# A four-layer graph network on one core: targets' positions and a zero in PSUM, a sort with a predicated copy held behind its group's messages, 64-row products in layer 2, and one 480-column product per slot in layer 2's sums

## The chip, the cores and the metric

The kernel runs on one core of a Trainium2 chip. One core has five engines with an instruction stream each: TensorE (PE; its weight loads are listed apart as PEld), VectorE (DVE), ScalarE (ACT), GpSimd (POOL, which here issues the indirect DMAs) and SyncE (SP, which here issues the direct DMAs). The metric is the device time of one launch in microseconds (us); "before" is the median of ten runs.

## The reference

A graph has N = 6250 nodes with 160 features each (64 scalars, 32 vectors of 3) and E = 100,000 edges, sorted by target `dst`. Four layers follow each other, each as `x = x + layer(relu(layernorm(x)))`. Layers 0, 1 and 3 gather by source and sum by target; layer 2 gathers by target and sums by source. Cut to what matters:

```python
# layers 0, 1 and 3 (W: small two-layer network of the edge's features)
w0, w1, w2, w3 = split(W(edge_features))
e0, e1 = h0[src], h1[src]                     # node features after a linear map
m0a = w0 * e0 * y0                            # y0, y1: edge_attr_4[:, :1], [:, 1:]
m0b = w3 * einsum('eui,ei->eu', e1, y1)
m1a = (w1 * e0)[:, :, None] * y1[:, None, :]
m1b = w2[:, :, None] * (e1 * y0[:, :, None])
n = segment_sum(concat(m0a, m0b, m1a, m1b), dst)      # 384 columns
# layer 2
sh1 = SQRT3 * edge_attr_3 / norm(edge_attr_3)
xs, xv = s[dst], v[dst]
out0a, out0b = w0 * xs, w3 * dot(xv, sh1)
out1a, out1b, out1c = w1 * xs * sh1, w2 * xv, w4 * cross(xv, sh1)
agg = segment_sum(concat(...), src)                   # 480 columns
```

After each sum stand linear maps of the nodes, in layer 2 a silu and a gate, in layer 3 a rotation by an angle.

## The kernel before

**Tiles.** An edge tile is 128 edges, one to a partition; there are TT = 784. WT = 14 tiles make a window (NW = 56 windows), two windows a unit (NU = 28 units), and up to G = 4 tiles a group, of which a layer has 196. Because edges are sorted by target, a window's edges reach few nodes. Within a window the even tiles hold the first half of its edges and the odd tiles the second half, so each kind reaches a run of under 64 nodes (HN = 64): a "half window".

**Prologue** (up to 165 us). `Fast.prologue` counts edges per bucket of sources, and writes tables that stay in SBUF: `self.loc` [128, 784], each edge's target relative to its half window's first node; `self.column`, for joining the two halves of a window; and `self.plus_w` (the line is `nc.vector.tensor_scalar(self.plus_w, pw[:, 0, :], iota_p, None, op0=ALU.add)`), for each window the node number that each of 128 partitions stands for.

**Layers 0, 1 and 3** are `edges(li)`, a loop over the 196 groups with work prepared ahead. For a group:

- SP loads per unit `rt` (attributes and source number of each edge, line 1236) and `ft` (edge features); POOL gathers the sources' rows from the table in HBM, one indirect DMA for each tile (L1277, 784 in a layer), six groups ahead into eight buffers `ge`.
- `hidden` and `edge_weights` make the weights: PE `ph` and `pw` (L1293 in layer 3, L1300 in layers 0 and 1), ACT copies them to `ws` (L1304, L1306).
- `messages` (L1309) is DVE's work: per unit one copy of three attribute rows into the PSUM tile `yls` (L1313); per group the comparison `oh` of an iota with `self.loc` (L1319), the products L1330, L1333, L1336, L1337 and L1338 and the reduction L1331. `msg` has 384 columns and 64 of scratch.
- PE multiplies `oh` (64 columns as weights) by `msg` and adds up in PSUM (`pg`, L1394), even tiles in the upper half of the partitions, odd ones in the lower. At the end of a window ACT copies `pg` out, and the generator `nodes` starts: `nodes_out` (L1051: ACT's copy `at` L1069, DVE's L1073 that carries the border of two windows, PE's `po` L1080 and L1082) and then `nodes_in` of the next layer (L982: norm, with `inv_sqrt` L966 to L975, maps, and the store of the next table rows). Each running generator is advanced by two steps in every group:

```python
            live = [n for n in live if not (next(n, True) or next(n, True))]
            if li < 2 and i % 3 == 0:
                next(self.sort, None)
```

**The sort.** Layer 2 needs each edge's place in the order of sources. `positions` (L1142) is a generator that makes it on DVE during layers 0 and 1, a step in every third group. For each of BK + 1 = 54 buckets it compares (L1166), scans with a running sum (L1168, over 784 columns, with the zeros `zeros_b` in SBUF as the second operand), yields, multiplies (L1171), adds (L1172) and yields. Whatever is left after layer 1 is run at once. The framework's scheduler orders each engine's instructions when it builds the program: by their place in it, but an instruction whose data and buffers are free by the scheduler's reckoning can be put ahead of others that wait. So the steps do not run just where they are written: from 388 us on the scans' starts lie 30 to 60 us apart through layer 0, then seven of them lie between 1583 and 1621 us, at the border to layer 1, and the next is at 1981.

**Layer 2, messages** are `messages2` (L1411). Per window `select` (L1438) loads on SP's queue 128 rows of the table, `tb` (L1443), from the window's first node on, whose number SP reads into a register (`self.at`), and the targets of its 1792 edges to all 128 partitions, `dt` (L1445), and compares them on DVE with `plus_w` (L1447) to the matrix `oh` [128 nodes, 14, 128 edges]. Per group PE makes `pw` (L1468, with 64 rows, from two halves of the partitions by turns) and gathers by a product, `pe` (L1479, one PSUM tile, one buffer):

```python
                nc.tensor.matmul(pe[:, k, :160], lhsT=oh[:, (t0 + k) % WT, :], rhs=tb, start=True, stop=True)
```

ACT copies `pe` to `ev` and `row` (L1484 to L1486) and two smaller pieces to `row` (L1487, L1488); DVE makes the rest of `row` (L1497 to L1506); POOL scatters each tile's 128 records of 390 numbers (1560 B) to `rec2` in HBM at the sorted places (L1509, 784 indirect DMAs). `row` has five buffers.

**Layer 2, sums** are `sums2` (L1543): for each of 53 buckets of 120 nodes, groups of up to 4 slots of 128 records. SP loads a group's records into `rt` [128, 4, 390] (L1570, 12 buffers, 8 groups ahead), DVE takes the places `loc` out of it (L1573), compares (`oh`, L1601) and makes 288 columns of `msg` (L1605, L1607); PE adds up 480 columns per slot in two products with the same weights:

```python
                nc.tensor.matmul(pg[:, 0:192], lhsT=oh[:, k, :], rhs=rt[:, k, 0:192], start=first, stop=end,
                                 skip_group_check=True)
                nc.tensor.matmul(pg[:, 192:480], lhsT=oh[:, k, :], rhs=msg[:, k, :], start=False, stop=end,
                                 skip_group_check=True)
```

These are L1611 and L1613; at a bucket's end ACT copies `pg` out by four copies (L1621 to L1624), and the node generators run as in the other layers.

## Time and profile before

| | us |
|---|---|
| median of 10 runs | 6640.2 |
| lowest, highest | 6571.16, 6687.38 |
| profiled execution, its own time | 6601.84 |
| its span, first to last instruction | 6600.0 |
| mean granted TensorE clock in it | 0.804 of full |

The stages follow each other almost without overlap, so the span can be cut at the times where one stage's lines end and the next one's begin: prologue 0 to 165, layer 0 to 1587, layer 1 to 3110, layer 2's messages to 4368, its sums to 5178, layer 3 to 6600. The profile has a row of digits for each engine over 40 slices of 165 us, the busy share in tenths; a line of TensorE's granted clock; and one of the traffic. The costliest groups of instructions are listed with line, engine, operation, tiles (out<-in) and count, then total busy us, mean ns of one, and the idle time just before them with what ended most of it. For example:

```profile
L1394 PE MATMUL pg<-msg,oh 128*64 128x384 f32 x4704 | 1190.1, 632 | 251.9 <-issue 114.4
L1337 DVE TENSOR_TENSOR msg<-msg,yls 128x768 f32<-128x768 f32 x588 | 554.9, 944 | 0.0
```

The first says that the 4704 passes of layers 0, 1 and 3's sums (two for each tile) kept PE busy for 1190.1 us, and that PE idled 251.9 us in front of them. The second, that DVE's product L1337 took 944 ns on average. A row of the timeline has the start in us, the length, engine, line, operation and tiles, and in brackets the idle time ahead of it with what ended it; "x8" there means eight instructions in one row.

### The profile page before, as it was taken

What the parts mean: (1) busy time and instruction counts of PE and PEld (TensorE: products, weight loads), DVE (VectorE), ACT (ScalarE), POOL (GpSimd) and SP (SyncE); (2) the same over time, 40 slices, a digit from 0 to 9 for tenths busy, and PEclk for the clock granted to TensorE, in tenths of its full rate; (3) what the DMA queues carried; (4) which work ended last, traced back from release to release, by engine and by line L of the source; (5) the groups of instructions that cost most, each with busy time, mean ns of one, the idle gap of its engine ahead of it and who ended that gap; (6) DMA issues with size and microseconds to landing.
All of it is one profiled execution on the core that took longest, in us unless ns stands there. A gap on an engine that the chain in (4) does not pass through costs nothing. (4 is left out here: it accounts for less than half of the span.)

```text
span 6600.0 us, 77043 instructions
## 1 busy us (share of the span) xinstructions
PE 5029.0 (76%) x22084; PEld 3072.0 (47%) x22084; DVE 4217.7 (64%) x11655; ACT 2084.0 (32%) x6858; POOL 3269.5 (50%) x3143
## 2 busy tenths in 40 slices
PE   6688888887678878776665666669999677877677
PEld 4344444444344444443443444458888433433333
DVE  5567777767456767555666666667777466655556
ACT  5333333333233333333333332312222233322222
POOL 0566666653555556552666766620000365555554
PEclk9788888877687788777777777789999777767777
DMA  3322222222222222222655555567777222222221
GB/s 89 95 74 69 72 71 73 69 57 59 60 70 75 72 70 77 69 60 66 226 197 190 202 191 193 179 229 249 236 235 233 67 67 63 64 61 59 61 58 40
DMA packets 371211, 733.89 MB, mean 111 GB/s; under 512 B 69677, under 2 KB 249098, under 8 KB 370650
## 3 DMA queue, kind: packets, MB, share of 16 engines
q0 software_dynamic: 163072, 349.43, 18.4%
q1 hardware_dynamic: 207122, 379.11, 18.3%
q8 instruction: 180, 2.95, 0.2%
q14 instruction: 253, 2.07, 0.1%
q10 hardware_dynamic: 584, 0.33, 0.0%
HBM read 519.59 MB, written 209.08 MB: 110 GB/s over the span
## 5 line engine op out<-in xcount | busy, mean ns | idle before, releaser
L1277 POOL DMA_INDIRECT ge<-table,rt x2352 | 2424.3, 1031 | 2823.8 <-DMA skip<-sk 829.1
L1394 PE MATMUL pg<-msg,oh 128*64 128x384 f32 x4704 | 1190.1, 632 | 251.9 <-issue 114.4
L1509 POOL DMA_INDIRECT rec<-row,edge_to x784 | 844.5, 1077 | 455.8 <-issue 249.7
L1304 ACT ACTIVATE ws<-pw,rt 128x96 f32<-128x96 f32 x2352 | 693.6, 347 | 1058.7 <-DVE msg L1338 214.2
L1300 PE MATMUL pw<-w_w2y,hh 100*128 100x192 f32 x3136 | 741.7, 379 | 142.4 <-ACT ws L1306 120.2
L1300 PEld LDWEIGHTS pw<-w_w2y,hh 100*128 100x128 f32 x3136 | 588.1, 219 | 406.6 <-ACT ws L1306 209.6
L1394 PEld LDWEIGHTS pg<-msg,oh 128*64 128x64 f32 x4704 | 335.7, 164 | 867.6 <-issue 505.2
L1073 DVE TENSOR_TENSOR at<-at 96x4 f32<-96x4 f32 x165 | 27.1, 164 | 907.6 <-ACT at L1069 769.1
L1479 PE MATMUL pe<-tb,oh 128*128 128x160 f32 x1568 | 377.5, 385 | 284.0 <-ACT row L1486 210.9
L1337 DVE TENSOR_TENSOR msg<-msg,yls 128x768 f32<-128x768 f32 x588 | 554.9, 944 | 0.0
L1266 PE MATMUL ph<-ft,w_w1r 12*100 12x512 f32 (+1 forms) x784 | 419.6, 713 | 160.7 <-ACT hh L1269 86.4
L1613 PE MATMUL pg<-msg,oh 128*120 128x288 f32 x1668 | 540.6, 405 | 0.0
L1479 PEld LDWEIGHTS pe<-tb,oh 128*128 128x128 f32 x1568 | 295.1, 241 | 457.5 <-ACT row L1486 309.8
L1269 ACT ACTIVATE hh<-ph 100x1024 f32<-100x1024 f32 (+1 forms) x336 | 268.5, 799 | 719.2 <-remote 208.8
L1333 DVE TENSOR_TENSOR msg<-ws,ge 128x512 f32<-128x512 f32 x588 | 400.8, 682 | 54.6 <-ACT ws L1306 54.6
L1611 PE MATMUL pg<-rt,oh 128*120 128x192 f32 x1668 | 409.3, 327 | 27.3 <-DMA rt<-rec 27.3
L1502 DVE TENSOR_TENSOR row<-pw,ev 128x512 f32<-128x512 f32 x196 | 135.1, 689 | 426.4 <-ACT row L1488 339.9
L1306 ACT COPY ws<-pw 128x192 f32<-128x192 f32 x1176 | 386.4, 329 | 0.0
L1611 PEld LDWEIGHTS pg<-rt,oh 128*120 128x120 f32 x1668 | 297.6, 183 | 115.3 <-issue 28.1
L1331 DVE TENSOR_REDUCE dot<-pr 128x128 f32<-128x384 f32 x588 | 343.0, 583 | 0.1
L1330 DVE TENSOR_TENSOR pr<-ge,yls 128x384 f32<-128x384 f32 x588 | 318.4, 541 | 29.0 <-DMA ge<-table,rt 25.0
L1293 PE MATMUL pw<-w_w2d,hh 64*128 64x192 f32 x1568 | 289.6, 404 | 47.8 <-remote 36.3
(486 smaller groups left out, 7729.5 us busy)
## 6 DMA issues: line engine op xcount, KB each, us to landing
rt<-rec SPq DMA_DIRECT2D x208, 780.0 KB
dt<-in_dst_w_dram SPq DMA_DIRECT2D x56, 896.0 KB
ge<-table,rt POOLq DMA_INDIRECT x2352
ft<-in_ft_dram SPq DMA_DIRECT2D x56, 512.0 KB
ft<-in_ft_dram SPq DMA_DIRECT2D x28, 896.0 KB
xt<-x SPq DMA_DIRECT2D x168, 82.0 KB
rec<-row,edge_to POOLq DMA_INDIRECT x784
rt<-in_rec_dram SPq DMA_DIRECT2D x84, 112.0 KB
```

The source lines that it names most:

```text
L1266: nc.tensor.matmul(ph[:, i], lhsT=w1[r : r + K, :], rhs=ft[r : r + K, 4 * P * (j // 2) :][:, : 4 * P], start=True, stop=True)
L1277: nc.gpsimd.indirect_dma_start(out=ge[:, k, :], out_offset=None, in_=self.table[li], in_offset=bass.IndirectOffsetOnAxis(ap=rt[:, G * g + ...
L1300: nc.tensor.matmul(pw[:, i, :192], lhsT=hh[:, k + i, :], rhs=w2, start=True, stop=True)
L1304: nc.scalar.activation(ws[:, k0 + i, 0:96], pw[:, i, 0:96], AF.Copy, scale=rt[:, G * g + k0 + i, 0:1])
L1306: nc.scalar.copy(ws[:, k0 : k0 + m, 96:192], pw[:, :m, 96:192])
L1333: tt(msg[:, :, AW - 64 : AW + 64].rearrange("p g (k u) -> p g k u", k=2), ws.rearrange("p g (k u) -> p g k u", k=2)[:, :, :, 0:64], e0[:, ...
L1337: tt(mvec[:, :, :, 0:64], by3(t1, 64), yv[:, :, :, None].to_broadcast([P, n, 3, 64]), ALU.mult)
L1394: nc.tensor.matmul(pg[half], lhsT=oh[:, k, :], rhs=msg[:, k, :AW], start=t % WT < 2, stop=t % WT >= WT - 2)
L1479: nc.tensor.matmul(pe[:, k, :160], lhsT=oh[:, (t0 + k) % WT, :], rhs=tb, start=True, stop=True)
L1509: d = nc.gpsimd.indirect_dma_start(out=self.rec2, out_offset=bass.IndirectOffsetOnAxis(ap=self.edge_to[:, t0 + k : t0 + k + 1], axis=0), i ...
L1611: nc.tensor.matmul(pg[:, 0:192], lhsT=oh[:, k, :], rhs=rt[:, k, 0:192], start=first, stop=end, skip_group_check=True)
L1613: nc.tensor.matmul(pg[:, 192:480], lhsT=oh[:, k, :], rhs=msg[:, k, :], start=False, stop=end, skip_group_check=True)
```

## The change

It touches every stage.

- **Prologue:** `plus_w` is computed so that partitions 0 to 63 stand for the 64 nodes from the first half window's first node on, and partitions 64 to 127 for those of the second half window.
- **Sort:** the scan's second operand is one zero in PSUM, read as a broadcast, and not `zeros_b` in SBUF. The multiplication and the addition become one copy under a predicate. A step is issued with `tc.issue_after(last.ins)`: its instructions stand behind the last message operation of the group in whose turn the step falls.
- **Layers 0, 1 and 3:** the PSUM tile of the attributes (now `bank`) has a fourth row per tile, the targets' places, copied once per unit; the comparison `oh` reads it there.
- **Layer 2's messages:** `select` makes two table loads of 64 rows and two target loads, of 896 edges to 64 partitions each, and one comparison of half as many columns. The products `pe` use 64 rows: even tiles the upper half of the partitions, odd tiles the lower. Slots of the PSUM tile are permuted, so that the two halves write to banks of their own; ACT's copies read through a view that undoes it.
- **Layer 2's sums:** `rt` has room for 288 columns in front of each record. The load lands behind them, DVE writes the messages into them, and one product of 480 columns takes the place of the two. ACT's copies at a bucket's end have other offsets.

```diff
-        nc.vector.tensor_scalar(self.plus_w, pw[:, 0, :], iota_p, None, op0=ALU.add)
...
+        nc.vector.scalar_tensor_tensor(self.plus_w, column, -1.0, pw[:, 0, :], op0=ALU.add, op1=ALU.add)
...
-            nc.vector.tensor_tensor_scan(cum, hit, self.zeros_b, self.off[:, b : b + 1], op0=ALU.add,
+            nc.vector.tensor_tensor_scan(cum, hit, self.zero.to_broadcast([P, TT]), self.off[:, b : b + 1], op0=ALU.add,
...
-            nc.vector.tensor_mul(cum, cum, hit)
-            nc.vector.tensor_add(pos, pos, cum)
+            nc.vector.copy_predicated(pos, hit.bitcast(mybir.dt.uint16), cum)
...
-    def at(self, k, most=N):
-
-        return self.nc.values_load(self.first[0:1, 2 * k : 2 * k + 1], engines=[mybir.EngineType.SP], min_val=0, max_val=most,
+    def at(self, k, most=N, half=0):
+
+        return self.nc.values_load(self.first[0:1, 2 * k + half : 2 * k + half + 1], engines=[mybir.EngineType.SP], min_val=0, max_val=most,
...
-        yls = p_y.tile([P, 2, 3, 2 * WT], F32, name="yls")
+        bank = p_y.tile([P, 8 * 2 * WT + 1], F32, name="bank")
+        yls = bank[:, : 8 * 2 * WT].rearrange("p (u c t) -> p u c t", u=2, c=4)
+        self.zero = bank[:, 8 * 2 * WT :]
+        nc.vector.memset(self.zero, 0.0)
...
-                nc.vector.tensor_copy(yl, rt[:, :, 1:4].rearrange("p t c -> p c t"))
+                nc.vector.tensor_copy(yl[:, 0:3], rt[:, :, 1:4].rearrange("p t c -> p c t"))
+                nc.vector.tensor_copy(yl[:, 3], self.loc[:, 2 * WT * u : 2 * WT * u + 2 * WT])
...
-            t0 = 2 * WT * u + G * g
...
-               self.loc[:, t0 : t0 + n, None].to_broadcast([P, n, HN]), ALU.is_equal)
+               yl[:, 3, gs, None].to_broadcast([P, n, HN]), ALU.is_equal)
...
-            yv = yl[:, :, gs].rearrange("p c t -> p t c")
+            yv = yl[:, 0:3, gs].rearrange("p c t -> p t c")
...
-            tt(mvec[:, :, :, 64:96], e1, by3(ws[:, :, 64:96], 32), ALU.mult)
-            return oh, msg
+            last = tt(mvec[:, :, :, 64:96], e1, by3(ws[:, :, 64:96], 32), ALU.mult)
+            return oh, msg, last
...
-            oh, msg = messages(u, g)
+            oh, msg, last = messages(u, g)
...
-                next(self.sort, None)
+                with tc.issue_after(last.ins):
+                    next(self.sort, None)
...
-            n = min(WT, TT - WT * k) * P
-            at = self.at(k)
...
-            nc.sync.dma_start(tb, self.table[2][ds(at, P), :])
-            dt = ld.tile([P, WT * P], I32, name="dt", bufs=2)
-            nc.sync.dma_start(dt[:, :n], self.a["dst_w"][k : k + 1, :n].to_broadcast([P, n]))
-            oh = ld.tile([P, WT, P], F32, name="oh", bufs=3)
-            nc.vector.tensor_scalar(oh.rearrange("p t e -> p (t e)")[:, :n], dt[:, :n], self.plus_w[:, k : k + 1], None,
+            dt = ld.tile([P, WT // 2 * P], I32, name="dt", bufs=2)
+            for h in range(2):
+                rows = slice(HN * h, HN * h + HN)
+                nc.sync.dma_start(tb[rows], self.table[2][ds(self.at(k, half=h), HN), :])
+                nc.sync.dma_start(dt[rows], self.a["dst_w"][2 * k + h : 2 * k + h + 1, :].to_broadcast([HN, WT // 2 * P]))
+            oh = ld.tile([P, WT // 2, P], F32, name="oh", bufs=3)
+            nc.vector.tensor_scalar(oh.rearrange("p t e -> p (t e)"), dt, self.plus_w[:, k : k + 1], None,
...
+
...
-                nc.tensor.matmul(pe[:, k, :160], lhsT=oh[:, (t0 + k) % WT, :], rhs=tb, start=True, stop=True)
+                h, rows = k % 2, slice(HN * (k % 2), HN * (k % 2) + HN)
+                nc.tensor.matmul(pe[:, 2 * h + k // 2, :160], lhsT=oh[rows, (t0 + k) % WT // 2, :], rhs=tb[rows],
+                                 start=True, stop=True)
+            pe = pe.rearrange("p (h t) c -> p t h c", h=2)
+            pair = lambda v: v.rearrange("p (t h) c -> p t h c", h=2)
...
-            pe = pe[:, :n]
...
-            nc.scalar.copy(ev[:, :, 0:160], pe[:, :, 0:160])
-            nc.scalar.copy(ev[:, :, 160:224], pe[:, :, 64:128])
-            nc.scalar.copy(row[:, :, 294:390], pe[:, :, 64:160])
+            nc.scalar.copy(pair(ev[:, :, 0:160]), pe[:, :, :, 0:160])
+            nc.scalar.copy(pair(ev[:, :, 160:224]), pe[:, :, :, 64:128])
+            nc.scalar.copy(pair(row[:, :, 294:390]), pe[:, :, :, 64:160])
...
-            rt = ld.tile([P, G, RW], F32, name="rt")
-            nc.sync.dma_start(rt[:, :m, :],
+            rt = ld.tile([P, G, 288 + RW], F32, name="rt")
+            nc.sync.dma_start(rt[:, :m, 288:],
...
-            nc.vector.tensor_scalar(loc[:, :m], rt[:, :m, 261], float(-BN * b), None, op0=ALU.add)
+            nc.vector.tensor_scalar(loc[:, :m], rt[:, :m, 288 + 261], float(-BN * b), None, op0=ALU.add)
...
-            rt = rt[:, :n]
+
+            msg, rt = rt[:, :n, 0:288], rt[:, :n]
+            row = rt[:, :, 288:]
...
-            msg = wk.tile([P, G, 288], F32, name="msg", bufs=3)[:, :n]
...
-            tt(msg[:, :, 0:192].rearrange("p g (c u) -> p g c u", c=3), by3(rt[:, :, 192:256], 64),
-               rt[:, :, 256:259, None].to_broadcast([P, n, 3, 64]), ALU.mult)
+            tt(msg[:, :, 0:192].rearrange("p g (c u) -> p g c u", c=3), by3(row[:, :, 192:256], 64),
+               row[:, :, 256:259, None].to_broadcast([P, n, 3, 64]), ALU.mult)
...
-               rt[:, :, 294:390].rearrange("p g (c u) -> p g c u", c=3), by3(rt[:, :, 262:294], 32), ALU.mult)
+               row[:, :, 294:390].rearrange("p g (c u) -> p g c u", c=3), by3(row[:, :, 262:294], 32), ALU.mult)
...
-                nc.tensor.matmul(pg[:, 0:192], lhsT=oh[:, k, :], rhs=rt[:, k, 0:192], start=first, stop=end,
-                                 skip_group_check=True)
-                nc.tensor.matmul(pg[:, 192:480], lhsT=oh[:, k, :], rhs=msg[:, k, :], start=False, stop=end,
-                                 skip_group_check=True)
+                nc.tensor.matmul(pg, lhsT=oh[:, k, :], rhs=rt[:, k, 0:480], start=first, stop=end)
...
-            nc.scalar.copy(vecs[:, :, 0:64], comp(192, 64))
-            nc.scalar.copy(vecs[:, :, 64:96], comp(384, 32))
-            nc.scalar.copy(vecs[:, :, 96:128], comp(0, 32))
-            nc.scalar.copy(acc[:, 384:480], pg[:, 96:192])
+            nc.scalar.copy(vecs[:, :, 0:64], comp(0, 64))
+            nc.scalar.copy(vecs[:, :, 64:96], comp(192, 32))
+            nc.scalar.copy(vecs[:, :, 96:128], comp(288, 32))
+            nc.scalar.copy(acc[:, 384:480], pg[:, 384:480])
...
-    a["dst_w"] = by_tile(i["dst"], 1 << 20).reshape(NW, WT * P)
+    a["dst_w"] = np.append(i["dst"], np.full(TT * P - E, 1 << 20, np.int32)).reshape(2 * NW, WT // 2 * P)
```

## The prediction

> **What bounds it now.** I read the page's head first, then busy time in six stretches cut where one stage's lines end and the next one's begin, then the groups of instructions, waits and timelines inside each stretch.
>
> ```profile
> PE 5029.0 (76%) x22084; PEld 3072.0 (47%) x22084; DVE 4217.7 (64%) x11655; ACT 2084.0 (32%) x6858; POOL 3269.5 (50%) x3143
> ...
> 165.00:1587.00 1422.00, 1166.62 (x5071) 655.67 (x5072) 988.93 (x2708) 518.30 (x1622) 840.21 (x784) 0.83 0.28 72
> 1587.00:3110.00 1523.00, 1184.41 (x4799) 649.79 (x4797) 926.79 (x2648) 518.34 (x1742) 806.06 (x784) 0.78 0.26 66
> 3110.00:4368.00 1258.00, 750.97 (x3356) 503.25 (x3356) 788.40 (x1627) 380.65 (x1092) 844.47 (x784) 0.75 0.55 193
> 4368.00:5178.00 810.00, 803.14 (x4276) 677.60 (x4276) 597.35 (x1774) 174.87 (x683) 0.00 (x0) 0.99 0.71 231
> 5178.00:6600.00 1422.00, 1012.73 (x4270) 514.90 (x4270) 818.62 (x2424) 408.76 (x1465) 778.06 (x784) 0.73 0.24 60
> ```
>
> The columns are the stretch, its length, then busy us of PE, PEld, DVE, ACT, POOL, the granted clock, the DMA share and GB/s. The rows are layer 0, layer 1, layer 2's messages, layer 2's sums and layer 3. No average limit holds for all. The sums are PE alone (803 of 810). In the messages POOL is busy 844 of 1258, and the space between its scatters is not counted as busy:
>
> ```profile
> L1509 POOL DMA_INDIRECT rec<-row,edge_to x784 | 844.5, 1077 | 455.8 <-issue 249.7 <-PE pw L1468 83.4 <-ACT row L1488 36.9
> ...
> 3595.18 0.97 POOL L1509 DMA_INDIRECT rec<-row,edge_to  x1 [0.30 <-issue]
> 3596.46 0.97 POOL L1509 DMA_INDIRECT rec<-row,edge_to  x1 [0.30 <-issue]
> 3608.26 0.97 POOL L1509 DMA_INDIRECT rec<-row,edge_to  x1 [10.82 <-ACT row L1488]
> ```
>
> Undisturbed, a scatter follows the last after 0.97 + 0.30 = 1.28 us, so 784 of them need 1003 us. From first to last they took 1217: 1003, plus 784 x (1077 - 974 ns) = 81 of stretched scatters, plus about 133 of starving like the 10.82 above (25 such gaps over 2 us). Before the first and after the last lie 41 us. That is the budget for this stage. In layers 0, 1 and 3 nobody is full: the engines wait for each other through the node chains (DVE at L1073 waited 769 us for ACT's copy L1069 in all).
>
> **Layer 2's sums: one product of 480 columns.** Two rows of the timeline price it:
>
> ```profile
> 4704.08 0.49 PE L1611 MATMUL pg<-rt,oh 128*120 128x192 f32 x2
> 4704.40 0.65 PE L1613 MATMUL pg<-msg,oh 128*120 128x288 f32 x2
> 4704.89 0.49 PE L1611 MATMUL pg<-rt,oh 128*120 128x192 f32 x2
> ...
> L1613 PE MATMUL pg<-msg,oh 128*120 128x288 f32 x1668 | 540.6, 405 | 0.0
> L1611 PEld LDWEIGHTS pg<-rt,oh 128*120 128x120 f32 x1668 | 297.6, 183 | 115.3 <-issue 28.1
> ```
>
> A product is two passes. From start to start the 192 columns take 0.32 us and the 288 take 0.49, so a slot is 0.81: per pass 162 and 243 ns, 0.84 ns a column and almost nothing fixed. 480 columns then take 0.403 a pass (the layers' 512 columns: 0.43) or 0.806 a slot. For 834 slots that is 3 us; the mean spacings with their stalls (164 and 246 ns, 0.82 a slot) give 13 at most. The 1668 weight loads that go lie beside the stream (PE idle ahead of L1613: 0.0), so they buy nothing. I take -4, from 0 to -13. The price is on the loads: records of 1560 B now land in steps of 2712 B instead of 6240 B in one run. In the trace's DMA records a 6240 B packet takes 238 ns (median), the scatters' 4680 B packets, three records each, 196, so four records are 261: +10%, and the stage's DMA share goes from 0.71 to 0.78. At the rate of the 640 B packets (32 ns) it would be 0.93. Loads run eight groups ahead, so I take 0; but DVE already waited 84 us for them at L1573, which leaves up to +30.
>
> **Layer 2's messages: row groups.** Products pe have 64 rows in place of 128, even tiles in the upper, odd in the lower half, with their own banks. The row with such halves is pw:
>
> ```profile
> 3614.98 1.03 PE L1468 MATMUL pw<-w_w2d,hh 64*128 64x224 f32 x8
> ...
> 3618.19 1.35 PE L1479 MATMUL pe<-tb,oh 128*128 128x160 f32 x8 [0.48 <-ACT row L1486]
> L1479 PE MATMUL pe<-tb,oh 128*128 128x160 f32 x1568 | 377.5, 385 | 284.0 <-ACT row L1486 210.9 <-ACT ev L1485 41.4 <-ACT ev L1484 11.0
> L1447 DVE TENSOR_SCALAR oh<-dt,plus_w 128x1792 f32<-128x1792 int32 x56 | 64.7, 1156 | 15.8 <-DMA dt<-in_dst_w_dram 15.7
> ```
>
> Eight passes of 224 columns start 97 ns apart, eight of pe's 160 columns 136 apart. At pw's rate pe's go to 69, and a group's eight from 1.08 to 0.55 us: 104 us of PE over 196 groups, nearly all in the shadow of POOL. Its path is the short loop pe, ACT's three copies, next pe (3.4 us where nothing holds it up, against POOL's 5.1 or more per group). So the gain is only in the 133 us of starving, where a faster loop refills five row buffers sooner. Its ends are 0 and -110; nearest to what the loop saves at the 25 gaps (two or three groups of 0.5 us each, 25 to 40) I take -35. The comparison L1447 halves: (1156 - 150)/1792 = 0.56 ns a column, so 0.65 us, 28 us of DVE, hidden. But it stretches POOL: scatters overlapping L1447 take 1463 ns on average where undisturbed ones take 973, 50 of them, 24 us; half goes: -12 (0 to -24). The target loads halve too (896 to 448 KB); at the start, where DVE waited 15.7 us for one, that may give 3. SP issues 168 more instructions that count (112 DMAs of 0.34 us and 56 register loads), 40 to 60 us spread over 1258 in a queue where only ft and the next window stand behind; 0. ACT's copies keep their elements. Together -50, from +20 (loads later) to -137.
>
> What speaks against halving the loads: the trace's 7168 B packets take 272 ns (median) where they fill 128 partitions and 446 in layer 3, where ft fills 16. The Trainium skill ("SBUF — State Buffer", Door 1) says that 64 partitions reach half of the ports, so no more bandwidth than 32. By the row, a half packet lies between 136 and 223 ns, so the loads' DMA time falls by 18 to 50%; by the rule it would not fall at all, the 3 us at the start would be 0, and the rest would stand.
>
> **Layers 0 and 1: the sort.** Per bucket, 54 in all, two passes of 965 ns (L1171, L1172) become one predicated copy that no row shows: between 0.36 us (the 784-wide comparison L1166) and 1.84 (the scan). The nearest row is the 965 of a pass with two inputs, so -52 us of DVE, from -5 to -85. The scan stays at 1.84: 2.3 ns an element is its own chain, and L1330, which reads PSUM, and L1338, which doesn't, take 545 and 550. Added are 84 copies of 28 targets' rows at 0.25 (below the 0.30 of L1313, above 0.14): +21. DVE gains 31 net, but idles 1029 us in these layers, and layer 1's groups took 7.2 us on average while the sort ran and 7.3 after its end: -4, from +10 to -40. The comparison L1319 stays at 0.41; it frees POOL's gathers a little (mean 1031, median 949), which wait for buffers anyway: 0.
>
> **Spreading the sort.** Seven buckets now run between the layers (scans from 1583 to 1621 us, then none until 1981), among the last node chain's small operations:
>
> ```profile
> 1595.18 1.84 DVE L1168 TENSOR_TENSOR_SCAN cum<-hit,off,zeros_b 128x784 f32<-128x784 bf16 x1
> 1596.94 0.13 DVE L970 TENSOR_SCALAR rstd<-rstd 128x1 int32<-128x1 int32 x1
> 1596.98 1.84 DVE L1168 TENSOR_TENSOR_SCAN cum<-hit,off,zeros_b 128x784 f32<-128x784 bf16 x1
> 1598.74 0.25 DVE L975 TENSOR_SCALAR rstd<-rstd 128x1 f32<-128x1 f32 x1
> ```
>
> From L992 (1594.38) to L888 (1605.10) this chain takes 10.7 us, of which its own twelve operations are 2.1; layer 1's first gathers wait for the table rows behind it. Held behind the last message operation of their own group, the buckets leave: -9 (0 to -25). They come back in layer 1's groups, where the rest of DVE's queue (node steps, the next group's messages) stands 2 to 3 us behind each: +3 (0 to +30), as above.
>
> **Sum.** -4 - 50 - 4 - 6 = -64 on the profiled execution's 6601.84 (span 6600.0): 6538. The ten runs' median is 6640.2, 0.6% above it; on it, -64 is **6576 us**. The forecast's own ends, all terms leaning one way within reason, are 6500 and 6625.
>
> **Rivals.** *The messages reach POOL's floor.* Starving and half the stretch vanish (-130), the sort gives its -40: with the rest about -180, **6460**. For it: PE, not POOL, holds the loop at the gaps, at a clock of 0.75. Against: the gaps come once in seven groups, not in every one. *It doesn't do what it says for the time:* weight loads, PE and DVE work all fall in shadow, scatters still at 1.28 us: **6635**. For it: the arithmetic of every term but one. *Slower: the sums become bound by DMA.* A group lasts 810/208 = 3.89 us and its DMA work 0.71 of that, 2.76. If a 1560 B run costs over 1.41 times its share of the long one (84 against 60 ns), loads set the pace; at 1.7 times, 4.69 us a group, 167 more, against -60 elsewhere: **6747**. Against: the scatters' 65 ns a record.
>
> **Chances.** Forecast 0.52, floor 0.18, nothing 0.20, DMA bound 0.10. A measurement here tells about 0.5%, 33 us, from no change: under 6607 is faster, over 6673 slower. The forecast gives 0.46 to faster and 0.06 to same, the floor 0.18 to faster, nothing 0.02, 0.17 and 0.01, DMA 0.10 to slower: 0.66, 0.23, 0.11. The range 6450 to 6670 leaves out the slow rival and the extremes.
>
> **What would show it.** Right: pe's eight passes in about 0.55 us; scatters' mean under 1.07 and their gaps' sum under 133; slots still 0.80 apart; no scans between L992 and L888 at the layers' border; the copy near 0.97. Wrong: PE waiting for rt in the sums, a messages stage still at 1258 or at 1120, a copy over 1.9, or layer 1's groups slower while the sort runs.

## The result, and the profile after

The changed kernel is slower: 6832.4 us median of 18 runs (6806.0 to 6926.3) against 6639.3 for the kernel before (62 runs). The ratio is 1.0298, 95% interval 1.0278 to 1.0318, where 0.990 was forecast. The profiled execution took 6829.4 us, span 6827.4, granted clock 0.778 (before: 0.804).

The page's first row, then the same columns as in the prediction (stretch, length, busy us of PE, PEld, DVE, ACT, POOL, granted clock, DMA share, GB/s) for layer 0, layer 1, the messages, the sums and layer 3, then three groups:

```profile
PE 5001.6 (73%) x20416; PEld 2763.1 (40%) x20416; DVE 4163.2 (61%) x11688; ACT 2082.3 (30%) x6858; POOL 3174.8 (47%) x3143
...
165.00:1610.00 1445.00, 1194.18 (x5044) 666.19 (x5044) 952.36 (x2675) 516.74 (x1618) 793.61 (x784) 0.83 0.27 70
1610.00:3255.00 1645.00, 1238.29 (x4826) 668.97 (x4824) 924.23 (x2687) 519.15 (x1746) 782.29 (x784) 0.75 0.24 63
3255.00:4518.00 1263.00, 600.98 (x3356) 408.08 (x3356) 764.15 (x1630) 382.54 (x1092) 832.78 (x784) 0.68 0.51 172
4518.00:5325.00 807.00, 800.38 (x2616) 406.23 (x2616) 606.30 (x1774) 170.91 (x683) 0.00 (x0) 0.99 0.76 232
5325.00:6827.00 1502.00, 1056.68 (x4264) 542.90 (x4262) 819.64 (x2448) 409.87 (x1464) 765.43 (x784) 0.70 0.23 57
...
L1516 POOL DMA_INDIRECT rec<-row,edge_to x784 | 832.8, 1062 | 472.6 <-issue 267.2
L1073 DVE TENSOR_TENSOR at<-at 96x4 f32<-96x4 f32 x165 | 26.9, 163 | 1167.3 <-ACT at L1069 1012.2
L1619 PE MATMUL pg<-rt,oh 128*120 128x480 f32 x1668 | 691.3, 567 | 37.2 <-DVE rt L1615 37.2
```

No engine got more to do: DVE and ACT are busy as long as before, within 2 us, or less (DVE in the sums 9 us more), POOL less in all stages; only PE's busy time in the layers is longer (1238 against 1184 us in layer 1), at a granted clock that is lower in layers 1 and 3 (0.75 against 0.78, and 0.70 against 0.73). Layer 1 is 122 us longer and layer 3 is 80 us longer all the same, and DVE's idle time ahead of L1073, the first DVE step of the node chain, rose from 907.6 to 1167.3 us. The row before was:

```profile
L1073 DVE TENSOR_TENSOR at<-at 96x4 f32<-96x4 f32 x165 | 27.1, 164 | 907.6 <-ACT at L1069 769.1
```

The stages that were rebuilt, messages and sums, hardly moved. So the loss is waiting, and it stands in layers where the forecast priced almost nothing.

For the rest of this text the stages are cut at events: the first gather of a layer, the first scatter, the first product of the sums, the end. The numbers come from two kinds of chips, which must be kept apart. The result comes from chips where the kernel before takes about 6640 us; most experiments got chips where the same kernel takes 5465 to 5474 ("quick chips" below), some got chips of the first kind (6630 and 6840, "late chips", for a reason that the section "One program on two chips" shows). Ratios are always to the kernel before on the same chip.

| us | late: before | late: changed | quick: before | quick: changed |
|---|---|---|---|---|
| layer 0 | 1452.6 | 1475.3 | 1162.2 | 1181.6 |
| layer 1 | 1518.3 | 1639.7 | 1129.7 | 1123.3 |
| layer 2, messages | 1226.0 | 1231.2 | 1100.4 | 1064.7 |
| layer 2, sums | 819.9 | 816.5 | 820.6 | 818.0 |
| layer 3 | 1411.3 | 1492.5 | 1070.7 | 1068.0 |

"Quick: before" is put together from two kernels that leave the stage as it was (e4_layer2 for layers 0 and 1, e3_issue for the rest). Each column comes from single traces, whose own times lie up to 38 us from the median of their kernel's runs. Two kernels that were traced again show layer 0 up to 23 us longer or shorter (e8_act 1135.5 and its repeat e15_act 1158.3; e6_no_loc 1123.6 and its repeats 1128.6 and 1106.1).

### The profile page after: what moved, and what is told of

Same layout as the page of the kernel before. It is cut to its first block, busy times and chain, and to the rows that moved or that the text cites. A ratio compares the mean times of both kernels' runs of the same rounds, so it can differ in the third digit from the quotient of the medians.

```text
span 6827.4 us, 74128 instructions
## 1 busy us (share of the span) xinstructions
PE 5001.6 (73%) x20416; PEld 2763.1 (40%) x20416; DVE 4163.2 (61%) x11688; ACT 2082.3 (30%) x6858; POOL 3174.8 (47%) x3143
## 5 line engine op out<-in xcount | busy, mean ns | idle before, releaser
L1279 POOL DMA_INDIRECT ge<-table,rt x2352 | 2341.3, 995 | 3130.1 <-DMA skip<-sk 826.5
L1396 PE MATMUL pg<-msg,oh 128*64 128x384 f32 x4704 | 1190.6, 632 | 148.0 <-issue 62.1
L1516 POOL DMA_INDIRECT rec<-row,edge_to x784 | 832.8, 1062 | 472.6 <-issue 267.2
L1073 DVE TENSOR_TENSOR at<-at 96x4 f32<-96x4 f32 x165 | 26.9, 163 | 1167.3 <-ACT at L1069 1012.2
L1619 PE MATMUL pg<-rt,oh 128*120 128x480 f32 x1668 | 691.3, 567 | 37.2 <-DVE rt L1615 37.2
L1396 PEld LDWEIGHTS pg<-msg,oh 128*64 128x64 f32 x4704 | 335.3, 165 | 801.9 <-issue 476.1
L1268 PE MATMUL ph<-ft,w_w1r 12*100 12x512 f32 (+1 forms) x784 | 480.7, 758 | 182.4 <-ACT hh L1271 113.6
L1339 DVE TENSOR_TENSOR msg<-msg,bank 128x768 f32<-128x768 f32 x588 | 555.1, 944 | 0.0
L1484 PE MATMUL pe<-tb,oh 64*128 64x160 f32 x1568 | 272.4, 410 | 370.7 <-ACT row L1493 195.9
L1484 PEld LDWEIGHTS pe<-tb,oh 64*128 64x128 f32 x1568 | 204.9, 254 | 519.0 <-ACT row L1493 304.7
L1333 DVE TENSOR_REDUCE dot<-pr 128x128 f32<-128x384 f32 x588 | 343.2, 584 | 0.1
L1340 DVE TENSOR_TENSOR msg<-ge,ws 128x384 f32<-128x384 f32 x588 | 323.3, 550 | 32.5 <-ACT ws L1306 32.5
L1295 PE MATMUL pw<-w_w2d,hh 64*128 64x192 f32 x1568 | 312.8, 428 | 40.9 <-remote 31.4
L1332 DVE TENSOR_TENSOR pr<-ge,bank 128x384 f32<-128x384 f32 x588 | 319.0, 543 | 28.0 <-DMA ge<-table,rt 18.3
```

The source lines that it names most:

```text
L1268: nc.tensor.matmul(ph[:, i], lhsT=w1[r : r + K, :], rhs=ft[r : r + K, 4 * P * (j // 2) :][:, : 4 * P], start=True, stop=True)
L1279: nc.gpsimd.indirect_dma_start(out=ge[:, k, :], out_offset=None, in_=self.table[li], in_offset=bass.IndirectOffsetOnAxis(ap=rt[:, G * g + ...
L1295: nc.tensor.matmul(pw[:, i, :192], lhsT=hh[r : r + 64, i, :], rhs=w2[r : r + 64, :], start=True, stop=True)
L1339: tt(mvec[:, :, :, 0:64], by3(t1, 64), yv[:, :, :, None].to_broadcast([P, n, 3, 64]), ALU.mult)
L1396: nc.tensor.matmul(pg[half], lhsT=oh[:, k, :], rhs=msg[:, k, :AW], start=t % WT < 2, stop=t % WT >= WT - 2)
L1484: nc.tensor.matmul(pe[:, 2 * h + k // 2, :160], lhsT=oh[rows, (t0 + k) % WT // 2, :], rhs=tb[rows], start=True, stop=True)
```

## The experiments

The change has five parts that can be put in alone: the places in PSUM (`loc`), the sort's copy under a predicate, with the scan's zero in PSUM (`sort`), its hold (`hold`), the 64-row products and the 480-column products (together `layer 2`). In the expectations quoted below, A, B and C are the theories of the first quotation, that of e1_loc; where a letter means something else, as in e5_whole, the quotation says what. Most expectations give numbers for both kinds of chips.

**One part each, on a quick chip (before 5468.0).**

e1_loc, the places in PSUM alone:

```diff
+                nc.vector.tensor_copy(yl[:, 3], self.loc[:, 2 * WT * u : 2 * WT * u + 2 * WT])
-               self.loc[:, t0 : t0 + n, None].to_broadcast([P, n, HN]), ALU.is_equal)
+               yl[:, 3, gs, None].to_broadcast([P, n, HN]), ALU.is_equal)
```

> The kernel before with one part alone: the targets' places copied to PSUM once per unit, and the comparison oh reading them there. Theory A (the order): the copy and the PSUM operand change how the scheduler lines up DVE's instructions in layers 0, 1 and 3, so that the node chain's L1073 stands in front of more of its group's message work and DVE waits longer there. Then this part alone carries most of the loss: layer 3 +80 us as in the changed kernel, layers 0 and 1 together +60 to +140, total 6780 to 6860. Theory B (the sort's hold): layers 0 and 1 lose by the sort's steps standing in front of the next group; then this part costs layer 3 alone, +60 to +90, total 6700 to 6730. Theory C (nothing in the layers, the clock falls because TensorE has less to do in layer 2): total 6630 to 6650.

Measured: 5490.0, ratio 1.0049 (1.0026 to 1.0071). The numbers expected were for the other kind of chip; layer 3 did not lose (1061.6), layer 0 did (1228.8 against 1162; this trace is the slowest of the kernel's runs, 36 us over their median).

e2_sort, the sort's copy alone:

```diff
-            nc.vector.tensor_mul(cum, cum, hit)
-            nc.vector.tensor_add(pos, pos, cum)
+            nc.vector.copy_predicated(pos, hit.bitcast(mybir.dt.uint16), cum)
```

> The kernel before with the sort's part alone: the scan's zero in PSUM and one copy under a predicate for the two passes; no hold behind the messages. By every theory the copy takes 1.03 us as in the changed kernel, 49 us less DVE work in all. Theory A: layer 1's order changes too, its price is not known beforehand: total 6610 to 6700, layer 3 unchanged within 10 us. Theory B: 6620 to 6645.

Measured: 5402.3, ratio 0.9893 (0.9848 to 0.9937): the largest gain of a part, 48 us in layer 0 and 22 in layer 1.

e3_issue, the hold alone:

```diff
+                with tc.issue_after(last.ins):
+                    next(self.sort, None)
```

> The kernel before with the hold alone: the sort's steps issued behind the last message operation of their group. Theory A: within 20 us of before (6620 to 6660), layer 3 unchanged. Theory B: layer 1 +80 to +130, layer 0 +20: total 6720 to 6790.

Measured: 5475.0, ratio 1.0022 (1.0002 to 1.0043). Theory B falls on this kind of chip: the hold costs next to nothing.

e4_layer2, the two products of layer 2:

```diff
+                nc.tensor.matmul(pe[:, 2 * h + k // 2, :160], lhsT=oh[rows, (t0 + k) % WT // 2, :], rhs=tb[rows],
+                                 start=True, stop=True)
...
+                nc.tensor.matmul(pg, lhsT=oh[:, k, :], rhs=rt[:, k, 0:480], start=first, stop=end)
```

> The kernel before with layer 2's parts alone: the 64-row products of the messages and the 480-column products of the sums. Theories A and B: messages +5, sums -3, the layers unchanged: 6630 to 6650. Theory C (a lower granted clock carries over into layer 3): layer 3 +60 to +80, total 6700 to 6720.

Measured: 5433.7, ratio 0.9946 (0.9927 to 0.9964): messages 1065.4 against 1100.4, sums 815.9 against 820.6, layer 3 unchanged (1071.0). Theory C falls on this kind of chip, although the messages' granted clock went from 0.80 to 0.70.

**The whole change, and all of it without the places in PSUM, on a quick chip (before 5469.0).**

> The changed kernel as it is, beside the kernel before on the chip that this call gets. The four parts alone were run on a chip where the kernel before takes 5468 us (and not 6640), and gave +22, -66, +7 and -34 us there. Theory A (the parts add up, and the loss of 193 us belongs to chips on which TensorE's results come late): where before takes about 5470, the whole change gives 5468 - 71, that is 5380 to 5420; where before takes about 6640 it gives 6810 to 6860 again. Theory B (the parts work against each other, the loss is in their sum): it is slower by 2 to 4% on every chip.

> The changed kernel without one part: the targets' places stay in SBUF. Theory A with the order of layer 3 as its price: where before takes about 5470, this gives 5360 to 5410 (22 us under the whole change); where before takes about 6640, layer 3 falls back from 1492 to about 1411 and the total is 6640 to 6750. Theory B': the loss lies in the sort's hold and the predicated copy: layer 3 falls back, but layer 1 stays over 1600, total about 6750.

Measured: 5425.1 and 5359.5; ratios 0.9920 (0.9901 to 0.9938) and 0.9805 (0.9775 to 0.9835). Here the change gains 0.8%, and would gain 2% without `loc`. Theory B of e5 falls: on this chip there is no loss. Theory A's 5380 to 5420 is missed by 5 us: `loc` costs 66 us beside the other parts, where it cost 22 alone. Of the 66 us between the two, layer 0 holds 58. There DVE's node steps show it, in e5_whole and then in e6_no_loc (idle time ahead of each in layer 0):

```profile
L1041 DVE TENSOR_TENSOR xt<-xt,pa 128x64 f32<-128x64 f32 x112 | 21.4, 233 | 109.4 <-ACT tb L1033 109.4
L1095 DVE SCALAR_TENSOR_TENSOR xt<-po,xt 128x64 f32<-128x64 f32 x56 | 15.8, 281 | 28.6 <-PE po L1082 28.6
```

```profile
L1041 DVE TENSOR_TENSOR xt<-xt,pa 128x64 f32<-128x64 f32 x112 | 21.6, 232 | 62.7 <-ACT tb L1033 62.7
L1095 DVE SCALAR_TENSOR_TENSOR xt<-po,xt 128x64 f32<-128x64 f32 x56 | 15.6, 279 | 18.2 <-PE po L1082 18.2
```

The instructions last as long; they stand at other places of DVE's queue and wait 57 us more there (47 and 10).

**What of `loc` costs, on a quick chip (before 5465.0).** Against the changed kernel, e7_sbuf copies the places to SBUF, e8_act lets ACT make the copy to PSUM, e9_unread keeps the copy and reads the places where they were:

```diff
-                nc.vector.tensor_copy(yl[:, 3], self.loc[:, 2 * WT * u : 2 * WT * u + 2 * WT])
+                nc.vector.tensor_copy(near[:, u % 2], self.loc[:, 2 * WT * u : 2 * WT * u + 2 * WT])
...
+                nc.scalar.copy(yl[:, 3], self.loc[:, 2 * WT * u : 2 * WT * u + 2 * WT])
...
-               yl[:, 3, gs, None].to_broadcast([P, n, HN]), ALU.is_equal)
+               self.loc[:, 2 * WT * u + G * g : 2 * WT * u + G * g + n, None].to_broadcast([P, n, HN]), ALU.is_equal)
```

> The changed kernel, but the targets' places are copied once per unit to a tile in SBUF, and not to PSUM; the comparison oh reads that. The copy and its place in the program stay; DVE's order comes out near that of the kernel without the copy (in layer 0 259 instructions of 2543 moved, against 661 for the changed kernel). On a chip where before takes about 5470 (whole change 5425, without the places in PSUM 5360): theory A (DVE's order is what costs) 5360 to 5390; theory D (the 84 copies and the wait of oh for them cost) 5410 to 5430. Where before takes about 6640: A 6640 to 6760, D 6800 to 6850.

> The changed kernel, but ACT copies the targets' places to PSUM in place of DVE; oh reads them in PSUM. In layer 3 DVE's order comes out near that of the kernel without the places in PSUM (237 of 2343 moved), in layers 0 and 1 near that of the changed kernel (240 and 473 moved). Theory A (order): layers 0 and 1 as in the changed kernel, layer 3 as without: where before takes about 5470, 5410 to 5440; where it takes about 6640, layer 3 about 1411 and 6730 to 6790. Theory E (the operand in PSUM costs by itself): all layers as in the changed kernel.

> The changed kernel with the copies to PSUM, but oh reads the places in SBUF as before: the copies have no reader. DVE's order is near that without them (179 of 2543 moved in layer 0). Theory A: 5360 to 5390 where before takes about 5470. Theory E: the same. Theory D in the form that the 84 copies cost by themselves: 5410 to 5430. Where before takes about 6640: A and E 6640 to 6760, D 6800 to 6850.

Measured: 5397.1, 5355.4 and 5364.8; ratios 0.9872 (0.9820 to 0.9925), 0.9824 (0.9767 to 0.9882) and 0.9824 (0.9777 to 0.9871). Theory E falls on quick chips: e8_act reads the places in PSUM and is as quick as e6_no_loc. Theory D falls: the copies without a reader cost nothing, and e7_sbuf, where the comparison waits for a copy, lies under D's 5410 to 5430. But theory A missed too: e7_sbuf and e8_act changed places against its numbers (layer 0 1164.7 and 1135.5), so counting how many instructions have moved does not tell what an order costs. In the repeats below the two kernels are alike in layer 0 (1162.7 and 1158.3); there the first lies in A's range and the second still misses it. What is left of A is that nearly the same work in another order costs 0 to 60 us in layer 0.

**Neither `loc` nor the hold, on a quick chip (before 5473.4).**

> The changed kernel without two parts: the targets' places stay in SBUF and the sort's steps are not held behind the messages. Left are the predicated copy with its zero in PSUM, the 64-row products and the 480-column products. On a chip where before takes about 5470: if the parts add up, 5468 - 66 - 34 = 5368, or 5350 to 5375 beside the 5360 with the hold; theory F (the hold is what makes the copy's gain possible, since DVE's order is the scheduler's) 5385 to 5410. Where before takes about 6640: 6600 to 6760.

Measured: 5358.0, ratio 0.9798 (0.9766 to 0.9830). Theory F falls; on a quick chip the hold is worth nothing either way.

**The two halves, on a late chip (before 6629.6).** e11_sorts has `sort` and `hold`, e12_rest has `loc` and `layer 2`.

> One half of the change: the kernel before with the sort's parts, the predicated copy with its zero in PSUM and the hold behind the messages. Where before takes about 5470: if the two add up, 5468 - 66 + 7 = 5409; theory F (they work on each other through DVE's order) anything from 5380 to 5440. Where before takes about 6640: theory A 6560 to 6680 with layer 3 unchanged at about 1411, theory B (these parts carry layer 1's loss) layer 1 over 1600 and a total over 6720.

> The other half: the kernel before with the targets' places in PSUM and layer 2's parts (64-row products, 480-column products), and the sort as before. Where before takes about 5470: if the parts add up, 5468 + 22 - 34 = 5456. With the other half (e11) it should then make the whole change's -44 us if the halves add up. Where before takes about 6640: theory A layer 3 at about 1492 and a total over 6720, theory B layer 1 at about 1520 and a total under 6720.

Measured: 6654.3 and 6841.4; ratios 1.0036 (1.0004 to 1.0067) and 1.0330 (1.0264 to 1.0395). The loss is back, and in the second half alone: layers 0, 1 and 3 1508.6, 1587.5 and 1481.3, against 1459.5, 1540.5 and 1391.5 in e11_sorts. Theory B falls here too. Of layer 1's loss e12_rest shows only 47 us, where the whole change lost 121.

**All but `loc` and `sort`, and all but `layer 2`, on another late chip (before 6839.6).** e13_iru has `hold` and `layer 2`, e14_sli has `loc`, `sort` and `hold`.

> The kernel before with the hold of the sort and layer 2's parts, without the targets' places in PSUM and without the predicated copy; DVE's order in layer 3 is that of before (8 of 2341 moved). Where before takes about 6640: theory A (the places in PSUM, by DVE's order, carry the loss) 6610 to 6670 with layer 3 at 1390 to 1420; theory C (layer 2's products lower the granted clock and the layers pay) over 6780. Where before takes about 5470: parts add up, 5468 + 7 - 34 = 5441.

> The kernel before with the sort's parts and the targets' places in PSUM, without layer 2's parts; DVE's order in layers 0, 1 and 3 is that of the changed kernel, instruction by instruction. Where before takes about 6640: theory A 6800 to 6850 with layer 3 at 1480 to 1500; theory C 6620 to 6670. Where before takes about 5470: the whole change's 5425 and 36 us more for the messages, that is 5455 to 5470.

Measured: 6813.7 and 7010.4; ratios 0.9961 (0.9933 to 0.9989) and 1.0205 (1.0150 to 1.0259). `loc` is what the two losing kernels have in common, and `layer 2` without it gains: theory C falls here as well. The stage was not the expected one. Layer 1 and layer 3 of e13_iru, then of e14_sli:

```profile
1659.00:3216.00 1557.00, 1188.72 (x4789) 642.62 (x4787) 933.37 (x2629) 513.43 (x1735) 816.76 (x784) 0.77 0.26 69
5278.00:6857.00 1579.00, 1077.06 (x4255) 550.55 (x4254) 813.89 (x2401) 404.09 (x1456) 772.75 (x784) 0.69 0.21 54
```

```profile
1687.00:3398.00 1711.00, 1272.53 (x4778) 683.32 (x4776) 917.87 (x2630) 513.57 (x1732) 781.18 (x784) 0.73 0.24 63
5470.00:7039.00 1569.00, 1066.99 (x4255) 551.56 (x4254) 815.61 (x2431) 406.56 (x1456) 761.28 (x784) 0.69 0.21 54
```

Layer 1 differs by 154 us, layer 3 hardly: on this chip layer 3 takes 1579 us with the old order too. DVE's busy time in layer 1 is 16 us less in the slower kernel. Both traces are of the longest run of their kernel, 45 and 31 us over the median.

**Four kernels again (before 5473.7, for e18_no_loc 5471.1).** e15_act is e8_act's kernel, e16_no_loc and e18_no_loc are e6_no_loc's, e17_sbuf is e7_sbuf's. Their expectations speak first of a late chip; they ran on quick ones.

> The changed kernel with ACT copying the targets' places to PSUM; the comparison oh reads them there. In layer 3 DVE's order is near that of the kernel without them (237 of 2343 moved). Where before takes 6600 or more: theory A (DVE's order carries the loss) layer 3 falls back by 60 to 100 us against the changed kernel's 1492, to near e16_no_loc's, and the total lies within 1% of before; theory E (the operand in PSUM carries it) layer 3 stays near 1490 and the total 2 to 3.5% over before. Where before takes about 5470 it repeats e8_act: about 5355.

> The changed kernel without the targets' places in PSUM. Where before takes 6600 or more: by theories A and E the loss is gone: within 1% of before, layer 3 at 1390 to 1420. Where before takes about 5470 it repeats e6_no_loc: about 5360.

> The changed kernel with the places copied by DVE to SBUF and read there. Where before takes 6600 or more: theory A layer 3 at 1390 to 1420 (its order there is near that without the places), the total within 1.5% of before; theory D (the copy and the wait for it) layer 3 at 1480 to 1500 and 2 to 3.5% over before. Where before takes about 5470 it repeats e7_sbuf: about 5397.

> The changed kernel without the targets' places in PSUM. Where before takes 6600 or more: theory A, from the halves (-0.4% for the hold with layer 2's parts, +0.4% for the sort's parts): within 0.7% of before. Theory C (layer 2's products carry part of the loss when the sort's parts are there too): 1 to 3% over before. Where before takes about 5470 it repeats e6_no_loc and e16_no_loc: about 5360.

Measured: 5369.4, 5361.9, 5383.3 and 5355.6; ratios 0.9796, 0.9792, 0.9826 and 0.9794, each within 0.003. They repeat the earlier ones within 14 us. The version without `loc` beats the kernel before on three quick chips, and the changed kernel on the one that ran both; on a late chip it was not run, nor was `loc` alone. Its halves' ratios there (0.9961 for e13_iru, 1.0036 for e11_sorts) let one expect no difference from before; that is an estimate.

## One program on two chips

The changed kernel was profiled on a late chip (the result) and on a quick one (e5_whole), with the same instructions in the same order. Here is the same place of layer 3, a window's end. First the late chip:

```profile
5989.19 1.51 PE L1396 MATMUL pg<-msg,oh 128*64 128x384 f32 x8 [0.94 <-issue]
...
5990.63 0.91 PE L1295 MATMUL pw<-w_w2d,hh 64*128 64x192 f32 x4
...
5992.09 0.94 DVE L1339 TENSOR_TENSOR msg<-msg,bank 128x768 f32<-128x768 f32 x1
...
5995.36 0.48 ACT L1399 COPY acc<-pg 128x384 f32<-128x384 f32 x1 [4.56 <-remote]
...
6002.49 0.58 ACT L1069 COPY at<-pt_out 96x512 f32<-96x512 f32 x1 [2.50 <-PE ph L1262]
6003.10 0.17 DVE L1073 TENSOR_TENSOR at<-at 96x4 f32<-96x4 f32 x1 [10.07 <-ACT at L1069]
6003.19 0.58 DVE L1333 TENSOR_REDUCE dot<-pr 128x128 f32<-128x384 f32 x1
...
6003.69 0.41 DVE L1321 TENSOR_TENSOR oh<-iota,bank 128x256 f32<-128x256 f32 x1
...
6004.02 0.28 DVE L1338 TENSOR_TENSOR msg<-ws,dot 128x128 f32<-128x128 f32 x1
```

Then the quick chip:

```profile
4818.85 1.51 PE L1396 MATMUL pg<-msg,oh 128*64 128x384 f32 x8 [0.89 <-DVE msg L1340]
...
4820.30 0.92 PE L1295 MATMUL pw<-w_w2d,hh 64*128 64x192 f32 x4
4820.44 0.48 ACT L1399 COPY acc<-pg 128x384 f32<-128x384 f32 x1
...
4821.77 0.94 DVE L1339 TENSOR_TENSOR msg<-msg,bank 128x768 f32<-128x768 f32 x1
4822.29 0.58 ACT L1069 COPY at<-pt_out 96x512 f32<-96x512 f32 x1 [0.66 <-PE pt_out L1062]
4822.90 0.16 DVE L1073 TENSOR_TENSOR at<-at 96x4 f32<-96x4 f32 x1 [0.20 <-ACT at L1069]
```

From the products pg (L1396) to DVE's L1339 the distances agree within 0.02 us (2.90 and 2.92). Then the quick chip's ACT copies pg 1.59 us after the products' start, and the late chip's 6.17 us after it, though both records show the passes issued alike. On the late chip TensorE's results are there later than its records say: the update of the semaphore that ACT waits for comes from TensorE at 5995.34, 4.6 us after the recorded end of the last product. In the traces of all six kernels from late chips, the one before included, 56 to 83 of the 168 copies of pg start more than 2 us after that recorded end; in the fourteen from quick chips none does. The recorded clock does not tell why: in this place it is full from 5982.7 to 5996.4 us. Over layer 3 it is lower on late chips (0.73 for the kernel before, 0.84 in e3_issue); whether that is a cause or comes of the waiting is not shown.

In the place shown ACT waits ("remote" means that no recorded instruction ended the wait), the copy `at` comes later still, and L1073 stands at the head of DVE's queue with the message work behind it: 10.07 us idle there, 0.20 here. Over the whole program this row's idle time is 1167.3 us on the late chip and 289.6 on the quick one; for the kernel before it is 907.6 on a late chip, and 202.4 on a quick one (e3_issue's row). So the change lengthens this wait by 87 us on a quick chip and by 260 on a late one. In layers 0, 1 and 3 DVE's other idle time falls by 50 us on the quick chip (428 to 378) and stays on the late one (733 and 737). There the 260 us, less 32 us of DVE work that went, are close to the 225 us that these layers grew. The rows of the kernel before on a quick chip (e3_issue's) and of the changed kernel on one (e5_whole's):

```profile
L1073 DVE TENSOR_TENSOR at<-at 96x4 f32<-96x4 f32 x165 | 26.8, 162 | 202.4 <-ACT at L1069 201.0
...
L1073 DVE TENSOR_TENSOR at<-at 96x4 f32<-96x4 f32 x165 | 26.7, 162 | 289.6 <-ACT at L1069 288.7
```

The order of DVE's queue in layer 3 shows what changed. Before, DVE's order at a unit's first window is L1331, L1333, L1336, L1337, then L1073, then L1338: one message operation of that group (0.55 us) waits behind L1073:

```profile
5748.03 0.58 DVE L1331 TENSOR_REDUCE dot<-pr 128x128 f32<-128x384 f32 x1
5748.53 0.68 DVE L1333 TENSOR_TENSOR msg<-ws,ge 128x512 f32<-128x512 f32 x1
5749.13 0.28 DVE L1336 TENSOR_TENSOR msg<-ws,dot 128x128 f32<-128x128 f32 x1
5749.33 0.95 DVE L1337 TENSOR_TENSOR msg<-msg,yls 128x768 f32<-128x768 f32 x1
5754.78 0.17 DVE L1073 TENSOR_TENSOR at<-at 96x4 f32<-96x4 f32 x1 [4.50 <-ACT at L1069]
5754.86 0.55 DVE L1338 TENSOR_TENSOR msg<-ge,ws 128x384 f32<-128x384 f32 x1
```

In the changed kernel L1073 stands ahead of the reduction L1333, the next group's L1321 and the product L1338 (0.58 + 0.41 + 0.28 us, line numbers of the changed kernel). This order stands at 26 of layer 3's 55 L1073, and on the late chip their waits add up to 245 us where the same 26 windows had 101 before; the waits at the others stay (287, before 300). So in this layer the longer wait stands where the order changed. That it costs the layer its 81 us is the reading that fits the result and e12_rest, and it is not shown: on the chip of e13_iru and e14_sli the same waits grow from 147 to 263 us and layer 3 takes no longer, and on quick chips they are 6 us in both kernels. The places in PSUM are the only part that touches this layer, and the kernels without them have the old order there.

## Why the prediction was wrong, step by step

- **The failed step** is in the part on the sort: "The comparison L1319 stays at 0.41; it frees POOL's gathers a little (mean 1031, median 949), which wait for buffers anyway: 0." Its durations came true (0.409 us; gathers' mean 995), and the edit still cost 66 us on a quick chip (e5_whole against e6_no_loc) and, by e12_rest and e14_sli, the two kernels with it that lost, 2 to 3.3% on late ones. The prediction priced every instruction and took the order of DVE's queue as given. The order is the scheduler's, and it changed in all three layers; in its place the runs show DVE's wait at L1073, 260 us longer on the late chip. That `loc` carries the loss there is shown by the four kernels of halves; that it does so by the order is argued. No rival had this mechanism; the slower one was about loads in the sums, which kept pace (DMA share 0.76).
- **"the engines wait for each other through the node chains"**, said of layers 0, 1 and 3, was right, and should have led to the question what stands behind L1073.
- **Messages, -50.** The starving was misread. The 25 gaps over 2 us between scatters (129.5 us) are a late chip's: e3_issue has none, and the shorter products left 30 (154.8 us) in the changed kernel. So the -35 for starving fell, and on the late chip the stage lost 5. The other part, the stretched scatters, came true on the late chip (mean 1077 to 1062 ns, 12 us, and -12 was forecast) and was undersized for quick ones: 1086 to 1041 ns, 784 x 45 ns = 35 us, that stage's whole gain there (36). Right: pe's passes start in pairs, 6 or 7 ns apart, one from each half of the rows; a group's eight then take 0.52 us from the first start to the last where they took 1.06 (the commonest value in each trace; medians 1.28 and 2.21), and L1447's comparison takes 0.69 us (0.65 forecast).
- **The loads' halves.** Packets of 3584 B take 140 ns (median) where 7168 B took 272, the lower end of the forecast. But a load is more than its packets. From the first packet to the end of the last, where no `ft` load runs beside it, a whole load took 3.43 us (median) and the two half loads together take 2.72; on quick chips 3.93 and 2.93 (e3_issue, e5_whole). So half the bytes take 0.75 to 0.8 of the time, at 169 GB/s in place of 267 on the late chip. The rule cited from the Trainium skill ("SBUF — State Buffer", Door 1) would have left the time as it was, at half the rate. The trace lies between; and since the two half loads are issued one after the other, it does not decide whether the rule applies here.
- **Sums, -4.** Right: 3.4 us less on the late chip, 4.7 in e4_layer2; passes 402 ns apart (403 forecast), 1560 B packets 66 ns (65 a record forecast from the scatters). DVE waits 131 us for records at L1580, 47 more than before, and in the stream PE does not wait for DVE; ahead of the first product it idles 37 us where it idled 27, since the one product needs DVE's messages too.
- **Sort, -4.** The copy takes 1.03 us (0.965 taken), the places' copies 0.18 (0.25 taken). The gain was undersized on quick chips: 66 us (e2_sort), more than the 49 us of DVE work that goes; on a late chip nothing (e11_sorts, with the hold, +0.4%). Layer 1's groups are nearer to 7.6 us, while the sort ran and after it, than to the 7.2 and 7.3 that were read; that they are alike holds.
- **Spreading, -6.** The last chain from L992 to L888 at the layers' border takes 2.3 us (1627.32 to 1629.61; 10.7 before) and has no scan in it, so the forecast 9 us are there; in time the hold is +7 us (e3_issue, on a quick chip), next to nothing.

What stays open: why some chips deliver TensorE's results late; which feature of the new order makes the kernel dearer there, since layers 1 and 3 lose 121 and 81 us in the result, 47 and 90 in e12_rest (against e11_sorts), and 153 and none in e14_sli (against e13_iru); and whether on a late chip the operand in PSUM costs something by itself, since the three kernels that could tell it (e15_act, e16_no_loc, e17_sbuf) ran on a quick chip only.

## What to carry to other kernels

Where a scheduler orders the queues, an edit that costs nothing by its durations can still move other work: compare the built order of each engine's queue before and after, and look at what stands behind the longest waits. Idle time that the records do not explain can be a delay of the chip that was traced; do not credit an edit with removing it. And a verdict from one chip may hold for that kind of chip only: the same program was 0.8% faster than before on one and 3% slower on the other.

## What the runs showed of the hardware

- Chips of two kinds: the kernel before takes 5465 to 5474 us on four, and 6630 to 6840 on others, with the same instructions. In the kernels run, the sums, where TensorE streams almost without a break, take 816 to 821 us on all of them; layer 3 takes 1051 to 1076 us on the quick ones and 1391 to 1579 on the others. On the late ones 56 to 83 of the 168 copies of pg start more than 2 us after the recorded end of TensorE's last product, on the quick ones none.
- The granted clock is recorded as half or full, in steps of 3.41 us. In the messages it fell from 0.80 to 0.70 on a quick chip when PE's busy time fell from 689 to 601 us (e3_issue, e4_layer2), and the stage still became 35 us shorter. The Trainium skill ("TensorE: Matmul & The Clock Gate", Part 1) says that recent activity decides between the two rates, which agrees. So in this stage the clock fell as the work got lighter, and that was no loss.
